# Two graph layers on one core: the last y tiles kept in SBUF, the first h turned in halves, the output stored by whole batches

## The chip, the core and the metric

The kernel runs on one core of a Trainium2 chip. The metric is the device time of one execution in microseconds. A core has TensorE (PE, with its weight loads shown as PEld), VectorE (DVE), ScalarE (ACT), GpSimd (POOL) and SyncE (SP); SP, ACT and POOL can issue DMAs. A tile in SBUF has 128 partitions; PE writes to PSUM banks of 128 x 512 float32.

## The reference

There are 16 graphs of 1024 nodes with 128 features, and a 0/1 adjacency matrix for each. Two blocks follow each other, both with a normalization in front and an addition of the input behind:

```python
# block 0: gated graph network, 4 layers
h = maximum(layernorm(x), 0)
for i in range(4):
    hw = h @ weight[i]                       # (b, n, c)
    m = einsum('bjn,bjd->bnd', adj, hw)      # sum over neighbours
    h = gru_cell(m, h, w_ih[i], w_hh[i], b_ih[i], b_hh[i])
x = x + h * nodemask
# block 1: graph convolution, 4 layers, batch norm over all batches and nodes
h = maximum(layernorm(x), 0)
for i in range(4):
    h = relu(einsum('bnm,bmc->bnc', adj, h @ W[i]) + b[i])
    mu, var = mean and variance of h over (b, n)
    h = gamma[i] * (h - mu) * rsqrt(var + 1e-5) + beta[i]
return x + h
```

In the GRU cell, r and z are sigmoids of sums of products with m and h, n is a tanh, and the new h is (1 - z) n + z h.

## The kernel before

The features lie transposed in SBUF, 128 features on the partitions and 1024 nodes along them. The large product, adjacency times features, is made exact enough by a split: a float32 operand is written as a high part, rounded to fp32r, and a low part, the rest; `aggregate_rows` (L523) multiplies both with each of eight rows of 128 nodes and accumulates in two PSUM banks. One batch and layer is 32 such matmuls of 128 x 512.

**Gated part.** Two streams, `sa` (even batches) and `sb` (odd), alternate by half steps: while one is in its gates, the other aggregates. Here every engine runs the instructions in the order in which they are written (`manual_schedule`). At the very start, batch 0's adjacency rows come by DMA and POOL (L562) or ACT (L560) rounds each one to fp32r; PE aggregates a row when it is rounded. In the same place the normalized y of batch 0 is turned by eight PE transposes into h (`turn`, L698, relu by ACT at L699), `open_gates` (L981) makes the first product with h, and `centred_high` (L779) writes the high part of the second half of y. A step of gates is `products` (L1011), `reset_gate` (r at L1029, DVE at L1030 and L1031), `candidate` (tanh, L1034), `update_gate` (z, L1038), `less`, `scaled` and `mixed` on DVE. In the first step `beside(0)` and `beside(1)` normalize and split batch 1 between them.

**Between the blocks.** For each batch the new x goes to DRAM (`store_xmid`, L743) and its normalized, rectified y too (`store_ymid`, L746). For the last two batches this work is done as chores during the first convolution layer: `chores` normalizes each stream's tile `s.xt` in place (L678) and stores it as y.

**Convolution part.** Outside `manual_schedule` the framework's scheduler orders the instructions. In layer 0, `load_y` (L1441) fetches a batch's y from DRAM into `feat[b]`, from batch 3 on behind a small POOL copy (L1440) that holds it back, and `first_split` splits it: ACT copies the high part (L1447), DVE subtracts (L1448). The split of batch b + 1 is issued while batch b aggregates. `first_weights` multiplies a batch's aggregate with the weights, `conv_done` applies bias and relu (L1421; in the last layer L1427) and takes the statistics (`bn_stats`, L1430). In layers 1 to 3 batch 0 is aggregated first on raw features (`raw_turned`, `raw_split`) while the factors of the batch norm are made (`affine`).

**Output.** In the last layer each relu writes `feat` in the order of the nodes, 256 elements an activation. `fetch_x` brings each x (L1530, POOL's queue) into 512-column halves of free tiles: the streams' tiles, the weights, and, at batch 15, the block of adjacency rows, one row tile and eight half tiles. The last loop normalizes a batch (L1643, L1647 or L1649), turns blocks of 128 columns on PE (L1655; nodes p * 4 + q of a half, a step of four columns), adds x on DVE (L1657) and stores each piece from SP (L1658). A piece of 512 nodes is one contiguous region of DRAM, 2 KB for each partition; batch 0 goes in pieces of 256, 256 and 512.

Of the kernel before, what the change touches and what calls it, by code (L numbers as in the profile page):

```python
# [8 lines left out]
F32 = mybir.dt.float32  # L9
F32R = mybir.dt.float32r  # L10
# [331 lines left out]
def exact_path(  # L342
# [36 lines left out]
    def acc(tag, name):  # L379
        return ps_m.tile([P, HALF], F32, tag=tag, name=name)  # L380

    def tmp(name):
        return ps_t.tile([P, HALF], F32, tag="tmp", name=name)
# [12 lines left out]
    def half_tile(name):  # L396
        return keep.tile([P, N], BF16, tag="half", name=name, bufs=8)
# [134 lines left out]
    with ExitStack() as st:  # L532
# [156 lines left out]
            norm_scale(nt, 0, NB)  # L689
            norm_blocks(xt, y, nt, range(NB))  # L690

        def turn(y, name, hT, func=AF.Copy):

            for hf in range(NH):
                pt = tmp(f"pt_{name}_{hf}")
                for q in range(BH):
                    k = hf * BH + q
                    nc.tensor.transpose(pt[:, q * P : (q + 1) * P], y[:, k * P : (k + 1) * P], ident)  # L698
                nc.scalar.activation(hT[:, hf * HALF : (hf + 1) * HALF], pt, func)  # L699
            return hT  # L700

        def by_nodes(cols):
            return cols.rearrange("c (q k i) -> c k q i", q=4, i=32)
# [39 lines left out]
        def store_ymid(b, y):  # L745
            nc.gpsimd.dma_start(ymid_d[b], y)  # L746
# [402 lines left out]
        with tc.manual_schedule(engines=every):  # L1149
# [53 lines left out]
            sa.centred_low(1)  # L1203
            for j in range(4):
                sa.rows[j] = first_round(0, j, raw0[j], nc.gpsimd)
            sa.agg_rows(range(4))
            for j in range(2):
                first_look(0, j, raw0[j])
            sa.rows[4] = first_round(0, 4, raw0[4], nc.scalar)
            sa.rows[5] = first_round(0, 5, raw0[5], nc.gpsimd)  # L1210
            turn(sa.y, "in0", h0, AF.Relu)
            sa.hT = h0
            first_look(0, 2, raw0[2])
            sa.agg_rows(range(4, 6))
            turn_small(*small_in)
            for j, eng in ((6, nc.scalar), (7, nc.gpsimd)):
                sa.rows[j] = first_round(0, j, raw0[j], eng)
            sa.open_gates()
            sa.agg_rows(range(6, NB))

            sb.sums(range(NB))
# [17 lines left out]
            def beside(hf):  # L1239
                sb.normed(range(hf * BH, (hf + 1) * BH))  # L1240
                sb.split_high(hf)
                sb.split_low(hf)
# [5 lines left out]

            sa.products(0)
            sa.reset_gate(0)  # L1250
            beside(0)
            in0 = turned_half(sb.y, h1, 0, "in1")
            exchange_in(in0, half_of(h1, 0))
            sa.candidate(0)
            sa.update_gate(0)
            sa.less(0)
            sa.scaled()
            beside(1)
# [154 lines left out]
    def conv_done(b, i, pm, stats, halfway=None):  # L1413
        for hf in range(NH):
            parts = 2 if halfway and hf else 1
            w = HALF // parts
            for k in range(parts):
                src = pm[hf][:, k * w : (k + 1) * w]
                if i < L - 1:
                    dst = feat[b][:, hf * HALF + k * w : hf * HALF + (k + 1) * w]  # L1420
                    last = nc.scalar.activation(dst, src, AF.Relu, bias=cvec(0, i))  # L1421
                else:
                    for q in range(w // (2 * P)):
                        u = hf * NH + k + q
                        dst = feat[b].rearrange("c (o j s i) -> c s o j i", o=2, j=4, s=4)[:, u]
                        part = src[:, q * 2 * P : (q + 1) * 2 * P].rearrange("c (j i o) -> c o j i", j=4, o=2)
                        last = nc.scalar.activation(dst, part, AF.Relu, bias=cvec(0, i))  # L1427
                    ks = slice(hf * NH + k, hf * NH + k + w // (2 * P))
                    dst = feat[b].rearrange("c (x s i) -> c x s i", s=4, i=32)[:, :, ks]
                nc.vector.bn_stats(stats[:, b * NH + hf + k, :], dst)  # L1430
            if halfway and hf == 0:
                sums = halfway()
        return sums if halfway else last
# [61 lines left out]
            nc.tensor.matmul(pc[hf], w_c[:, i, :], mt[:, cols], start=True, stop=True)  # L1495
        conv_done(0, i, pc, stats)

    xo = []

    def pieces(b):  # L1500

        return [(0, HALF // 2), (HALF // 2, HALF // 2), (HALF, HALF)] if b == 0 else [(0, HALF), (HALF, HALF)]

    def by_node(d, n0, n):

        return d[n0 : n0 + n, :].rearrange("(p q) c -> p q c", p=P)

    def xo_piece(b, n0, n):
        return xo[b][n0 // HALF][:, n0 % HALF : n0 % HALF + n].rearrange("p (q c) -> p q c", c=C)

    def fetch_x(b):

        first = len(xo)
        if b == 2:
            ts = [flat(f"xo{k}").rearrange("p k c -> p (k c)") for k in range(4)]
            hs = [t[:, k * HALF : (k + 1) * HALF] for t in ts for k in range(2)]
            for t in (w_hhT, w_mT):
                t = t.rearrange("p l c -> p (l c)")
                hs.extend(t[:, k * HALF : (k + 1) * HALF] for k in range(3))
        elif b == B - 1:  # L1520
            wide = turned_tile("xo_wide").rearrange("p a n -> p (a n)").bitcast(F32)
            row = keep.tile([P, N], F32, tag="row", name="xo_row", bufs=12)
            hs = [t[:, k * HALF : (k + 1) * HALF] for t, n in ((wide, 8), (row, 2)) for k in range(n)]
            hs.extend(half_tile(f"xo_h{k}").bitcast(F32) for k in range(8))
        else:
            return
        xo.extend(hs[k : k + 2] for k in range(0, len(hs), 2))
        for k in range(first, len(xo)):
            for n0, n in pieces(k):
                nc.gpsimd.dma_start(xo_piece(k, n0, n), by_node(xmid_d[k], n0, n))  # L1530

    def chores(s, b):

        xt, parts = s.xt, feat[b]
        y = xt.rearrange("p k c -> p (k c)")
        nt = norm_tiles(f"mid{b}")

        def sums(q):
            ks = range(2 * q, 2 * q + 2)
            masked_sum(b, xt, parts, ks)  # L1540
            norm_sums(xt, nt, ks)

        def factors():
            norm_factors(nt)
            store_xmid(b, xt)

        def blocks(hf):
            norm_blocks(xt, y, nt, range(hf * BH, (hf + 1) * BH))

        def fetch(seen):  # L1550
            nc.gpsimd.tensor_copy(parts[:, :1], seen[:, :1].bitcast(F32))
            pair_in(s.pair, parts, nc.gpsimd)

        return [
            (0, fetch),
            *((1 + q, lambda seen, q=q: sums(q)) for q in range(4)),
            (4, lambda seen: factors()),
            (6, lambda seen: blocks(0)),
            (7, lambda seen: blocks(1)),
            (7, lambda seen: store_ymid(b, y)),  # L1560
        ]

    late = {}
# [8 lines left out]
    for b in range(B):  # L1572
        if b == 1:
            with tc.issue_after(sb.last_dve.ins):
                rows = load_adjT(b, 0)
        else:
            rows = load_adjT(b, 0)
        yt = load_y(b + 1, hw_last if b > 2 else None) if b + 1 < B else None
        pm = banks(b, 0)
        aggregate(pm, hw, rows, 0)  # L1580
        behind = first_weights(*waiting, stats) if waiting else sb.last_m
        hw_next = first_split(b + 1, yt, behind) if b + 1 < B else None
        with tc.issue_after(split[0].ins), tc.issue_after(split[1].ins):
            for go in late.get(b, ()):
                go(hw[1])
        if b == B - 1:
            hw_next = raw_split(1)
        aggregate(pm, hw, rows, 1)
        if b == 12:
            raw_turned(1)  # L1590
        if b == 2:
            nc.gpsimd.dma_start(degree, degree_d.partition_broadcast(P))
        hw_last, hw, waiting = hw, hw_next, (b, pm)
# [46 lines left out]
    for b in range(B):  # L1640
        hT = work.tile([P, N], F32, tag="h", name=f"bn{b}_{L}", bufs=3)
        if b > 1:
            nc.scalar.activation(hT, feat[b], AF.Identity, bias=aff[1], scale=aff[0])  # L1643
        for n0, n in pieces(b):
            cols = slice(n0, n0 + n)
            if b == 0 and n0 == 0:
                nc.vector.tensor_scalar(hT[:, cols], feat[b][:, cols], aff[0], aff[1], ALU.mult, ALU.add)  # L1647
            elif b < 2:
                nc.scalar.activation(hT[:, cols], feat[b][:, cols], AF.Identity, bias=aff[1], scale=aff[0])  # L1649
            tag = turns[count % len(turns)]  # L1650
            count += 1
            pt = (tmp(f"pt_o{b}_{n0}") if tag == "tmp" else acc(tag, f"pt_o{b}_{n0}"))[:, :n]
            some = hT[:, n0 : n0 + n].rearrange("c (p q) -> c q p", p=P)
            for q in range(n // P):
                nc.tensor.transpose(pt[:, q * P : (q + 1) * P], some[:, q, :], ident)  # L1655
            xh = xo_piece(b, n0, n)
            nc.vector.tensor_add(xh, pt.rearrange("p (q c) -> p q c", c=C), xh)  # L1657
            nc.sync.dma_start(by_node(out[b], n0, n), xh)  # L1658


@with_exitstack
# [49 lines left out]
```

## Time and profile before

| what | value |
|---|---|
| median of 3 runs | 1768.21 us (1767.53 to 1768.83) |
| the profiled execution | 1769.41 us |
| its span, first to last instruction | 1767.6 us |
| mean granted PE clock | 0.996 |
| busy: PE, PEld | 1744.3 us (99%), 1185.0 us (67%) |
| busy: DVE, ACT, POOL | 1323.2, 1148.2, 398.2 us |
| DMA | 375.50 MB, mean 212 GB/s |

The gated part lasts until about 1150 us, the four convolution layers until about 1736 us, the output until the end. The busy time of PE is modelled from pipelined matmuls, so the waits of PE, the granted clock and the starts of successive matmuls say more than its share. A name such as `feat<-ymid_d` means that `feat` is written from `ymid_d`; "x16" counts instructions; what stands in brackets is the idle time before an instruction and what ended it.

### The profile page before, as it was taken

To read this page: it belongs to the slowest core of one execution; us is meant where nothing else is said; L and a number is where in the kernel's file an instruction comes from. 1 tells how busy PE (TensorE), PEld (TensorE's weight loads), DVE (VectorE), ACT (ScalarE), POOL (GpSimd) and SP (SyncE) were. 2 spreads that over 40 slices of the span, in tenths; PEclk is the share of its full clock that TensorE was granted. 3 is DMA by queue.
4 is the path that set the end of the run, shared out by engine and by line. 5 is a ranking of instruction groups with operands and counts; after the bars stand their busy time and mean duration, and the time that the engine had idled before them with its cause. 6 is when DMAs were issued, how large, how long until landed. Compare 5 with 4: busy or idle time off the path is not lost. (4 is left out here: it accounts for less than half of the span.)

```text
span 1767.6 us, 22191 instructions
## 1 busy us (share of the span) xinstructions
PE 1744.3 (99%) x6654; PEld 1185.0 (67%) x6654; DVE 1323.2 (75%) x2378; ACT 1148.2 (65%) x1821; POOL 398.2 (23%) x451
## 2 busy tenths in 40 slices
PE   9999999999999999999999999999999999999997
PEld 5665656565656565656656565677678888888886
DVE  7777887887887887887888686767566666666665
ACT  6567556657556656565655664468677778768765
POOL 4314223232341331331422423122200001000010
PEclk9999999999999999999999999999999999999999
DMA  8458379468557656746846836899957667757566
GB/s 287 128 139 275 101 159 289 118 172 257 160 161 213 196 154 193 238 129 178 259 122 172 288 102 182 270 323 323 344 178 238 236 241 238 261 204 265 212 236 254
DMA packets 305313, 375.50 MB, mean 212 GB/s; under 512 B 24876, under 2 KB 189520, under 8 KB 305184
## 3 DMA queue, kind: packets, MB, share of 16 engines
q1 hardware_dynamic: 292864, 334.06, 60.1%
q0 software_dynamic: 11792, 39.68, 7.0%
q8 instruction: 54, 0.88, 0.2%
q14 instruction: 75, 0.61, 0.1%
q10 hardware_dynamic: 528, 0.26, 0.0%
HBM read 272.19 MB, written 101.72 MB: 212 GB/s over the span
## 5 line engine op out<-in xcount | busy, mean ns | idle before, releaser
L523 PE MATMUL pm<-row,ghw 128*128 128x512 f32 x2048 | 504.2, 403 | 0.5 <-POOL row L562 0.3
L523 PEld LDWEIGHTS pm<-row,ghw 128*128 128x128 f32 x2048 | 383.8, 188 | 107.6 <-issue 23.7
L523 PE MATMUL pc_m<-wide,chw 128*128 128x512 f32 x1024 | 245.4, 395 | 0.0
L523 PEld LDWEIGHTS pc_m<-wide,chw 128*128 128x128 f32 x1024 | 190.5, 188 | 42.6 <-issue 4.3
L972 ACT COPY m<-pm 128x512 f32<-128x512 f32 x128 | 68.7, 588 | 229.6 <-PE pm L523 229.6
L587 POOL CAST row<-stage 128x1024 fp32r<-128x1024 f32 x112 | 127.4, 1143 | 339.3 <-DMA stage<-in_adj_dram 117.7
L523 PE MATMUL pc_g_r<-wide,chw 128*128 128x512 f32 x464 | 189.0, 407 | 6.5 <-ACT chw L1447 6.5
L523 PE MATMUL pc_g_z<-wide,chw 128*128 128x512 f32 x464 | 182.2, 393 | 0.0
L1030 DVE SCALAR_TENSOR_TENSOR r<-g_hn,vecs,r 128x512 f32<-128x512 f32 x128 | 93.4, 730 | 108.6 <-ACT r L1029 56.7
L633 POOL CAST pair<-row 128x1024 bf16<-128x1024 f32 x128 | 165.6, 1344 | 32.8 <-DVE adjT L639 32.8
L1034 ACT ACTIVATE r<-r,vecs 128x512 f32<-128x512 f32 x128 | 92.2, 720 | 115.5 <-DVE r L1031 113.3
L1368 DVE CAST wide<-block 128x1024 fp32r<-128x1024 bf16 x160 | 110.2, 694 | 68.4 <-PE pc_m L523 40.0
L1368 DVE CAST wide<-packed 128x1024 fp32r<-128x1024 bf16 x160 | 109.1, 689 | 62.9 <-PE pc_g_z L523 45.1
L1366 ACT CAST wide<-packed 128x1024 fp32r<-128x1024 bf16 x96 | 100.6, 1049 | 50.0 <-PE pc_m L523 20.8
L1011 PE MATMUL g_r<-m,w_mT 128*128 128x512 f32 x256 | 130.8, 592 | 0.1
L1011 PE MATMUL g_xn<-m,w_mT 128*128 128x512 f32 x256 | 130.7, 592 | 0.0
L1011 PE MATMUL g_z<-m,w_mT 128*128 128x512 f32 x256 | 130.7, 592 | 0.0
L1366 ACT CAST wide<-block 128x1024 fp32r<-128x1024 bf16 x96 | 100.5, 1048 | 43.7 <-PE pc_g_z L523 25.7
L1029 ACT ACTIVATE r<-g_r,brz 128x512 f32<-128x512 f32 x128 | 88.0, 687 | 58.2 <-PE g_r L1011 57.8
L1430 DVE BATCH_NORM_STATS2 stats<-feat 128x6 f32<-128x512 f32 x129 | 85.7, 684 | 49.0 <-ACT feat L1421 35.4
L1051 DVE TENSOR_TENSOR h<-h,z 128x512 f32<-128x512 f32 x128 | 95.2, 744 | 17.3 <-ACT z L1038 5.0
L1047 DVE TENSOR_TENSOR h<-h,r 128x512 f32<-128x512 f32 x96 | 72.0, 750 | 47.6 <-ACT r L1034 47.0
(202 smaller groups left out, 2904.0 us busy)
## 6 DMA issues: line engine op xcount, KB each, us to landing
block<-adjT_d SPq DMA_DIRECT2D x256, 256.0 KB, 4.7
packed<-adjT_d SPq DMA_DIRECT2D x256, 256.0 KB, 5.7
stage<-in_adj_dram SPq DMA_DIRECT2D x120, 512.0 KB, 5.2
adjT_d<-adjT SPq DMA_DIRECT2D x64, 512.0 KB, 7.2
cross_h<-t_h SPq DMA_DIRECT2D x94, 256.0 KB, 2.1
n_h<-cross_h SPq DMA_DIRECT2D x376, 64.0 KB, 2.1
xmid_d<-x POOLq DMA_DIRECT2D x16, 512.0 KB, 3.8
x<-in_x_dram SPq DMA_DIRECT2D x15, 512.0 KB, 4.4
```

The source lines that it names most:

```text
L523: nc.tensor.matmul(pm[hf], hw[s][:, j * P : (j + 1) * P], rows[j][:, hf * HALF : (hf + 1) * HALF], start=(j == 0 and s == 0), stop=(j == N ...
L587: nc.gpsimd.tensor_copy(t, stage[j % 4])
L633: nc.gpsimd.tensor_copy(halves[:, :, o], rows[4 * o + j].bitcast(F32))
L1011: nc.tensor.matmul(po, wT[:, i, g * C : (g + 1) * C], rhs, start=start, stop=stop)
L1029: nc.scalar.activation(r, pr, AF.Sigmoid, bias=brz[:, 3 * i : 3 * i + 1])
L1030: nc.vector.scalar_tensor_tensor(r, phn, b_hn(i), r, ALU.add, ALU.mult)
L1034: nc.scalar.activation(self.r, self.r, AF.Tanh, bias=b_in(self.i))
L1047: nc.vector.tensor_sub(ho, hin, self.r)
L1051: nc.vector.tensor_mul(ho, ho, self.z)
L1366: nc.scalar.copy(r, t)
L1368: nc.vector.tensor_copy(r, t)
L1430: nc.vector.bn_stats(stats[:, b * NH + hf + k, :], dst)
```

## The change

**y of the last two batches.** `store_ymid` is taken from the chores of batches 14 and 15, and `first_split` of these two reads the stream's own tile, in which y was made, in place of `feat[b]` loaded from DRAM. Batches 0 to 13 are as before.

**First h in halves.** `turn` becomes `turn_half`. PE's order at the start was rows 0 to 3, eight transposes, rows 4 and 5, the small transposes, `open_gates`, rows 6 and 7. It becomes rows 0 and 1, four transposes, row 2, `open_gates`, row 3, four transposes, rows 4 and 5, the small transposes, rows 6 and 7. On ACT the first relu of h now follows `centred_high(1)` directly and stands ahead of row 4's rounding. In the first step of gates z is computed right behind the reset gate, ahead of `beside(0)`, where it stood behind the candidate.

**Output in whole batches.** The relu of the last layer writes node p * 8 + r to column r * 128 + p, so its inner run of writes has a step of 128 elements (512 bytes), and `bn_stats` reads runs of four. The transposes then read 128 neighbouring columns. A partition holds 8 neighbouring nodes, 4 KB in DRAM. For batches 2 to 4 and 6 to 14 x is fetched and the result is stored with one DMA of 512 KB, after both halves are added; batches 0, 1, 5 and 15 still go in pieces, which are now parts (1 or 2 KB of each 4 KB run) of a batch. The tiles for x of batches 7 to 15 become four parts of the adjacency block, four row tiles and one split tile (`hw00`).

```diff
@@ start
+            sa.hT = h0
+            sa.agg_rows(range(2))
+            turn_half(sa.y, "in0", h0, 0, AF.Relu)
+            sa.agg_rows(range(2, 3))
+            sa.open_gates()
+            sa.agg_rows(range(3, 4))
-            sa.agg_rows(range(4))
...
-            turn(sa.y, "in0", h0, AF.Relu)
-            sa.hT = h0
+            turn_half(sa.y, "in0", h0, 1, AF.Relu)
...
-            sa.open_gates()
             sa.agg_rows(range(6, NB))
...
             sa.reset_gate(0)
+            sa.update_gate(0)
             beside(0)
...
             sa.candidate(0)
-            sa.update_gate(0)
             sa.less(0)
@@ conv_done, last layer
-                        dst = feat[b].rearrange("c (o j s i) -> c s o j i", o=2, j=4, s=4)[:, u]
-                        part = src[:, q * 2 * P : (q + 1) * 2 * P].rearrange("c (j i o) -> c o j i", j=4, o=2)
+                        dst = feat[b].rearrange("c (r o j s h) -> c s o j h r", r=8, o=2, j=4, s=4)[:, u]
+                        part = src[:, q * 2 * P : (q + 1) * 2 * P].rearrange("c (j h r o) -> c o j h r", j=4, r=8, o=2)
                         last = nc.scalar.activation(dst, part, AF.Relu, bias=cvec(0, i))
@@ output pieces
+    def whole(b):
+        return xo_whole[b] is not None and 1 < b < B - 1
+    def by_node(d, q0, n):
+        return d.rearrange("(p q) c -> p q c", p=P)[:, q0 : q0 + n, :]
@@ fetch_x
+            ts += [w3[:, :N], None, m3[:, HALF : 3 * HALF]]
...
+            ts = [wide[:, k * N : (k + 1) * N] for k in range(4)]
+            ts += [row_tile(f"xo_row{k}").bitcast(F32) for k in range(4)]
+            ts.append(keep.tile([P, N], F32R, tag="hw00", name="xo_hw").bitcast(F32))
...
+            if whole(k):
+                nc.gpsimd.dma_start(xo_whole[k].rearrange("p (q c) -> p q c", c=C), by_node(xmid_d[k], 0, NB))
+                continue
@@ chores
-            (7, lambda seen: store_ymid(b, y)),
@@ layer 0
-        yt = load_y(b + 1, hw_last if b > 2 else None) if b + 1 < B else None
+        if b + 1 < B - 2:
+            yt = load_y(b + 1, hw_last if b > 2 else None)
+        elif b + 1 < B:
+            yt = (sa if b + 1 == B - 2 else sb).xt.rearrange("p k c -> p (k c)")
@@ output loop
-            some = hT[:, n0 : n0 + n].rearrange("c (p q) -> c q p", p=P)
-            for q in range(n // P):
-                nc.tensor.transpose(pt[:, q * P : (q + 1) * P], some[:, q, :], ident)
+            for q in range(n):
+                nc.tensor.transpose(pt[:, q * P : (q + 1) * P], hT[:, (q0 + q) * P : (q0 + q + 1) * P], ident)
...
+            if not whole(b):
+                nc.sync.dma_start(by_node(out[b], q0, n), xh)
+        if whole(b):
+            nc.sync.dma_start(by_node(out[b], 0, NB), xo_whole[b].rearrange("p (q c) -> p q c", c=C))
```

More of the change, by code (lines that the diff above doesn't have):

```diff
@@ L690, in norm_apply, with turn_half @@
             norm_blocks(xt, y, nt, range(NB))
[L692 to L700, printed above, removed]
+        def turn_half(y, name, hT, hf, func=AF.Copy):
+            pt = tmp(f"pt_{name}_{hf}")
+            for q in range(BH):
+                k = hf * BH + q
+                nc.tensor.transpose(pt[:, q * P : (q + 1) * P], y[:, k * P : (k + 1) * P], ident)
+            nc.scalar.activation(hT[:, hf * HALF : (hf + 1) * HALF], pt, func)
         def by_nodes(cols):
@@ L1424, in conv_done @@
                         u = hf * NH + k + q
-                        dst = feat[b].rearrange("c (o j s i) -> c s o j i", o=2, j=4, s=4)[:, u]
-                        part = src[:, q * 2 * P : (q + 1) * 2 * P].rearrange("c (j i o) -> c o j i", j=4, o=2)
+                        dst = feat[b].rearrange("c (r o j s h) -> c s o j h r", r=8, o=2, j=4, s=4)[:, u]
+                        part = src[:, q * 2 * P : (q + 1) * 2 * P].rearrange("c (j h r o) -> c o j h r", j=4, r=8, o=2)
                         last = nc.scalar.activation(dst, part, AF.Relu, bias=cvec(0, i))
                     ks = slice(hf * NH + k, hf * NH + k + w // (2 * P))
-                    dst = feat[b].rearrange("c (x s i) -> c x s i", s=4, i=32)[:, :, ks]
+                    dst = feat[b].rearrange("c (x s h) -> c x s h", s=4, h=4)[:, :, ks]
                 nc.vector.bn_stats(stats[:, b * NH + hf + k, :], dst)
@@ L1496, in raw_weights, with xo_piece @@
         conv_done(0, i, pc, stats)
-    xo = []
+    xo, xo_whole = [], []
     def pieces(b):
[L1502 to L1509, printed above, removed]
+        return [(0, 2), (2, 2), (4, 4)] if b == 0 else [(0, 4), (4, 4)]
+    def whole(b):
+        return xo_whole[b] is not None and 1 < b < B - 1
+    def by_node(d, q0, n):
+        return d.rearrange("(p q) c -> p q c", p=P)[:, q0 : q0 + n, :]
+    def xo_piece(b, q0, n):
+        return xo[b][q0 // BH][:, q0 % BH * C : (q0 % BH + n) * C].rearrange("p (q c) -> p q c", c=C)
     def fetch_x(b):
@@ L1515, in fetch_x @@
             ts = [flat(f"xo{k}").rearrange("p k c -> p (k c)") for k in range(4)]
[L1516 to L1519, printed above, removed]
+            w3, m3 = (t.rearrange("p l c -> p (l c)") for t in (w_hhT, w_mT))
+            ts += [w3[:, :N], None, m3[:, HALF : 3 * HALF]]
+            apart = [w3[:, N : 3 * HALF], m3[:, :HALF]]
         elif b == B - 1:
             wide = turned_tile("xo_wide").rearrange("p a n -> p (a n)").bitcast(F32)
-            row = keep.tile([P, N], F32, tag="row", name="xo_row", bufs=12)
-            hs = [t[:, k * HALF : (k + 1) * HALF] for t, n in ((wide, 8), (row, 2)) for k in range(n)]
-            hs.extend(half_tile(f"xo_h{k}").bitcast(F32) for k in range(8))
+            ts = [wide[:, k * N : (k + 1) * N] for k in range(4)]
+            ts += [row_tile(f"xo_row{k}").bitcast(F32) for k in range(4)]
+            ts.append(keep.tile([P, N], F32R, tag="hw00", name="xo_hw").bitcast(F32))
         else:
             return
-        xo.extend(hs[k : k + 2] for k in range(0, len(hs), 2))
+        for t in ts:
+            xo_whole.append(t)
+            xo.append([t[:, :HALF], t[:, HALF:]] if t is not None else apart)
         for k in range(first, len(xo)):
-            for n0, n in pieces(k):
-                nc.gpsimd.dma_start(xo_piece(k, n0, n), by_node(xmid_d[k], n0, n))
+            if whole(k):
+                nc.gpsimd.dma_start(xo_whole[k].rearrange("p (q c) -> p q c", c=C), by_node(xmid_d[k], 0, NB))
+                continue
+            for q0, n in pieces(k):
+                nc.gpsimd.dma_start(xo_piece(k, q0, n), by_node(xmid_d[k], q0, n))
     def chores(s, b):
@@ L1643, in exact_path @@
             nc.scalar.activation(hT, feat[b], AF.Identity, bias=aff[1], scale=aff[0])
-        for n0, n in pieces(b):
-            cols = slice(n0, n0 + n)
-            if b == 0 and n0 == 0:
+        for q0, n in pieces(b):
+            cols = slice(q0 * P, (q0 + n) * P)
+            if b == 0 and q0 == 0:
                 nc.vector.tensor_scalar(hT[:, cols], feat[b][:, cols], aff[0], aff[1], ALU.mult, ALU.add)
@@ L1651, in exact_path @@
             count += 1
-            pt = (tmp(f"pt_o{b}_{n0}") if tag == "tmp" else acc(tag, f"pt_o{b}_{n0}"))[:, :n]
-            some = hT[:, n0 : n0 + n].rearrange("c (p q) -> c q p", p=P)
-            for q in range(n // P):
-                nc.tensor.transpose(pt[:, q * P : (q + 1) * P], some[:, q, :], ident)
-            xh = xo_piece(b, n0, n)
+            pt = (tmp(f"pt_o{b}_{q0}") if tag == "tmp" else acc(tag, f"pt_o{b}_{q0}"))[:, : n * P]
+            for q in range(n):
+                nc.tensor.transpose(pt[:, q * P : (q + 1) * P], hT[:, (q0 + q) * P : (q0 + q + 1) * P], ident)
+            xh = xo_piece(b, q0, n)
             nc.vector.tensor_add(xh, pt.rearrange("p (q c) -> p q c", c=C), xh)
-            nc.sync.dma_start(by_node(out[b], n0, n), xh)
+            if not whole(b):
+                nc.sync.dma_start(by_node(out[b], q0, n), xh)
+        if whole(b):
+            nc.sync.dma_start(by_node(out[b], 0, NB), xo_whole[b].rearrange("p (q c) -> p q c", c=C))
 @with_exitstack
```

## The prediction

> **What bounds the kernel now.** I read the list of waits of TensorE (PE) first. PE is busy for 1744.3 of 1767.6 us, so a change pays where PE waits, at the very start, or after its last instruction. Columns: who waits, on what, us in total, times, longest.
>
> ```profile
> PE pc_g_r L523 <- ACT chw L1447: 6.5, 1, 6.5
> PE pt_idle L1156 <- POOL ident masks.py:199: 2.4, 1, 2.4
> PE pt_wm L488 <- ACT w_both L482: 0.7, 1, 0.7
> PE g_z L1011 <- ACT z L1038: 0.6, 1, 0.6
> ```
>
> Two belong to the change: a single wait of 6.5 us for the split `chw` of L1447, and 0.6 us for the update gate `z`. The first I followed through the timelines of PE, ACT and POOL (start, length, engine, line, what; in brackets the idle time before):
>
> ```profile
> 1265.62 1.04 ACT L1447 CAST chw<-feat 128x1024 fp32r<-128x1024 f32 x1
> 1266.56 1.65 ACT L678 ACTIVATE x<-x,ms_mid,rs_mid 128x128 f32<-128x128 f32 x4
> 1268.51 1.02 POOL L746 DMA_DIRECT2D ymid_d<-x  x1 [8.71 <-ACT x L678]
> 1278.14 0.53 POOL L1441 DMA_DIRECT2D feat<-ymid_d  x1 [8.62 <-DMA ymid_d<-x]
> 1283.11 1.04 ACT L1447 CAST chw<-feat 128x1024 fp32r<-128x1024 f32 x1 [8.36 <-DMA feat<-ymid_d]
> 1273.46 4.24 PE L523 MATMUL pc_m<-wide,chw 128*128 128x512 f32 x16
> 1284.21 0.80 PE L523 MATMUL pc_g_r<-wide,chw 128*128 128x512 f32 x1 [6.51 <-ACT chw L1447]
> ```
>
> L1447 runs 16 times; the one at 1283.11 is batch 15's. Its y is finished in SBUF at 1268.2, goes out to DRAM (9.6 us), comes back (5.0 us), and only then is split. Batch 14's split, at 1265.62, is on time. Stages of the granted clock (columns: stretch, us, busy us of PE, PEld, DVE, ACT, POOL, then PEclk, DMA share, GB/s) show a second cost, PE at half speed after the wait:
>
> ```profile
> 1283.00:1284.00 1.00, 0.00 (x0) 0.00 (x0) 0.00 (x0) 0.89 (x1) 0.00 (x0) 0.50 0.05 20
> 1286.00:1288.00 2.00, 2.00 (x6) 1.54 (x5) 1.84 (x4) 2.00 (x4) 0.00 (x0) 0.50 0.00 0
> 1289.00:1290.00 1.00, 1.00 (x5) 0.81 (x4) 0.30 (x2) 0.00 (x0) 0.00 (x0) 0.85 0.00 0
> ```
>
> The same table for the output, and the DMA queue's packets in 1744 to 1760 and, behind, for one lone ymid store in 1089.3 to 1096:
>
> ```profile
> 1738.00:1740.00 2.00, 2.00 (x12) 1.66 (x12) 1.68 (x4) 2.00 (x3) 0.00 (x0) 1.00 0.39 131
> 1746.00:1748.00 2.00, 2.00 (x16) 1.82 (x15) 2.00 (x5) 2.00 (x3) 0.00 (x0) 1.00 1.01 379
> 1758.00:1760.00 2.00, 0.00 (x0) 0.00 (x0) 0.15 (x1) 0.00 (x0) 0.00 (x0) 1.00 1.02 378
> q1 hardware_dynamic: 3218, 5.85, 97.8%
> q0 software_dynamic: 144, 0.52, 19.7%
> ```
>
> The DMA engines have room until about 1744, then none until about 1761; DVE makes its last addition at 1758.2. So the end is set by the rate of the output stores.
>
> **y of the last two batches.** Two stores, two loads and two 0.24 us gate copies on POOL go; the splits read the tile where y was normalized. Batch 14's round trip is hidden and gains nothing. For batch 15 y is ready at 1268.2, and ACT is free after the relu that ends at 1274.75. With the cadence of the batches before (split 9.02 us after the last one) it starts at 1274.64; DVE's low part follows 1.34 us later and takes 1.22 (till 1277.20). PE wants it, by the step from 1255.41 to 1259.49 two batches earlier, at 1273.46 + 4.08 = 1277.54. It came at 1284.21: 6.67 us late. Eleven steps of the matmuls behind it, 1284.21 to 1289.40, took 5.19 us; at the usual 0.2275 us they take 2.50. So 2.69 us more went on the clock, 9.36 together.
>
> What is late next? Rows: the casts for (layer 1, batch 1) come 9.36 earlier, at 1284.45; their loads are issued by 1275.6 and landed within a median 7.9 us, 1283.5, with the round trip's traffic still beside them. raw_split reads loads issued before 1248. POOL's two fetches into the streams' tiles now wait for the splits (1268.2, 1277.2); queued behind is at most raw_split's load, some 2 us of delay if the order fell badly. I take 9.36, bounds 8.0 and 9.6.
>
> The Trainium skill ("TensorE: Matmul & The Clock Gate", section "Part 1: The HAM clock gate") lets a throttled clock recover after about 3.4 us of sustained work. By that the slow stretch would cost about 1.7 us and the sum would be 1 us smaller; the rows here show the half clock for 4.9 us, and I keep them.
>
> **The head.** Nothing is added; eight transposes, two relus and one product move, and `z` passes ahead of batch 1's first half. PE now idles between rows 0 to 3 (casts on POOL end 1.28 us apart), and the four transposes (about 0.5 us) fit there. But the first relu of h stands on ACT behind a relu that waits for DVE:
>
> ```profile
> 13.62 0.63 ACT L779 ACTIVATE ghw<-y_in 128x512 fp32r<-128x512 f32 x1 [2.90 <-DVE y_in L773]
> 20.42 1.07 ACT L972 COPY m<-pm 128x512 f32<-128x512 f32 x2 [3.09 <-PE pm L523]
> ```
>
> So open_gates cannot start before 14.15 + 0.55 = 14.7. PE is through with row 2 at about 13.3 and waits 1.45 us, with row 3 (13.56 before) queued behind. Row 3 then comes at 15.6, 2.04 later; 0.5 (transposes) and 0.86 (g_hn, two halves of 0.43) are done by then, leaving some 0.6 us late; I take 0.5 for the end of the sum. ACT works without a gap from 20.4 to 38.4, so all of it shifts by 0.5. Against that, PE's 0.6 us of waiting for `z` goes: `z` follows `r`. Its 0.67 us is then in front of batch 1's norm and splits, needed for row 4 at about 34.1, where the low split would end at about 34.0. Batch 1's `m` copies follow ACT's 0.5, with 0.23 us of slack. Net: 0.1 us gained, bounds 0.9 gained (if the relu of h isn't late) and 0.8 lost. The gap of 1.45 us costs no clock: after 1756.4 PE was idle over 3.5 us before the clock fell.
>
> **The last relu.** 64 activations write with a step of 512 bytes. No ACT row of before has one. Now they take 0.475 us (256 elements; 0.213 per 256 by L1643 against L1649, the rest fixed). The nearest rows are mild: ACT's L1401 reads every second element at 856 against L1649's 800 ns, PE's L1655 loads weights with a step of 16 bytes at 210 against L498's 191. I take a tenth, 0.05 each; bounds nothing and, at four times the element time, 0.64. Beside PE this is hidden: in 1610 to 1720 ACT is busy 7.02 us per batch of 9.09. On the path lie the last two: 0.1, at most 1.3. bn_stats reads whole runs still; nothing.
>
> **The output.** Per packet: 0.978 x 16 x 16.0 us / 3218 = 77.8 ns at 2 KB, 0.197 x 16 x 6.7 / 144 = 147 ns at 4 KB. A 256 KB piece (144 packets with its semaphores) holds the engines for 0.70 us, a whole batch in 4 KB runs for 1.32 instead of 1.40. Twelve batches go whole (2 to 4, 6 to 14): 0.96 us gained. Batch 2's first bytes wait for its second half, one addition of 0.61, while the engines have room: lost. Net 0.35 gained; bounds 1.9 gained (packets at the 440 GB/s of single slots) and 0.6 lost (no faster at all). PE's transposes now read without a step, SP issues 21 stores for 33, the fetches of x become fewer and start until 1727; DVE's additions and the queue cover them, and x arrives some 8 us before use.
>
> **Sum.** 9.36 + 0.1 + 0.35 - 0.1 = 9.7. The profiled execution took 1769.41 (span 1767.6 and 1.8 around it): 1759.7. It stood 1.20 above the median of 1768.21, so **1758.5**.
>
> **Rivals.**
> - *The wait moves.* Batch 15's split gets a new neighbour on ACT, or row casts come late: a wait of 2 to 3 us, too short for the clock to fall. For: the stage is replanned, DMA is 0.99 busy in 1268 to 1276. Against: the margins above. 1761.
> - *The relu becomes ACT's bound, and no gain is left.* At four times the element time (1.11 us) ACT needs 2.56 more per batch with 2.07 free: 0.49 x 15 = 7.4, plus 1.3 at the end: 1767.1.
> - *The same, and slower.* It decides beyond 1.19 us an activation: 15 x (4d - 2.07) + 2d reaches 13.2 us, the gain and 0.2%, at d = 0.71. At five times (1.33 us) it takes 20 + 1.7 us: 1780. For: nothing shows that step on ACT. Against: steps of 8 and 16 bytes cost 7 to 11%.
> - *It doesn't do what it says:* another wait of the same length holds batch 15's split. Nothing else of it is unfinished at 1274; 1768.
>
> The Trainium skill ("Advanced Engine Details and Errata", section "SBUF Cachelines") says that accesses which hit a new 16-byte line each time pay a penalty. That is the rule by which the relu rivals would come; it gives no size, and the 16-byte step on PE cost 19 ns of 191.
>
> **Numbers.** Forecast 0.82, moved wait 0.08, relu without gain 0.03, relu slower 0.04, no effect 0.03. Bounds added up give 1755.8 to 1762.4; the range is 1755.5 to 1763.5. About 0.2% (3.5 us) is what can be told from no change: faster 0.90, same 0.06, slower 0.04.
>
> **What would show it.** PE's wait for L1447 is gone and the clock stays at 1.00 near 1277. L1427 stays near 0.5 us. PE waits about 1.4 us for h near 13.3, and not for `z`. Output packets are 4 KB, and the last store lands 5 to 6 us after DVE's last addition, as before. I am wrong if the split still waits, if L1427 passes 1 us, or if the head grows by over 1 us.

## The result and the profile after

| | before | after |
|---|---|---|
| median of 5 runs | 1768.21 us (1767.53 to 1768.86) | 1759.38 us (1758.68 to 1760.17) |
| ratio | | 0.995, interval 0.9936 to 0.9965 |
| the profiled execution, its span | 1769.41, 1767.6 us | 1759.38, 1757.6 us |
| mean granted PE clock | 0.996 | 0.998 |

The change makes the kernel faster by 8.83 us (interval 6.2 to 11.3). The profiled pair differs by 10.0 us. PE's list of waits, after (who waits, on what, us in total, times, longest):

```profile
PE pt_idle L1152 <- POOL ident masks.py:199: 2.4, 1, 2.4
PE g_hn L977 <- ACT h_in L698: 1.4, 1, 1.4
PE pt_wm L488 <- ACT w_both L482: 0.7, 1, 0.7
```

The 6.5 us for the split is gone, and so is the 0.6 us for `z`. A wait of 1.4 us for the first half of h is new. The timelines of ACT and PE, after (start, length, engine, line, what; in brackets the idle time before; L1446 is L1447 of before, L977 is in `open_gates`):

```profile
1274.04 1.04 ACT L1446 CAST chw<-x 128x1024 fp32r<-128x1024 f32 x1
1272.85 4.24 PE L523 MATMUL pc_m<-wide,chw 128*128 128x512 f32 x16
1276.93 0.39 PE L523 MATMUL pc_g_r<-wide,chw 128*128 128x512 f32 x1
1285.96 1.98 PE L523 MATMUL pc_m<-wide,chw 128*128 128x512 f32 x8
14.65 1.13 PE L977 MATMUL g_hn<-h_in,w_hhT 128*128 128x512 f32 x2 [1.36 <-ACT h_in L698]
21.08 1.07 ACT L968 COPY m<-pm 128x512 f32<-128x512 f32 x2 [2.36 <-PE pm L523]
```

Batch 15's split now reads `x`, the stream's own tile, at 1274.04, where it ran at 1283.11. PE goes from batch 14's last 16 matmuls to batch 15's first in 1276.93 - 1272.85 = 4.08 us, with no idle time. The fourth line is the start of layer 1: 13.11 us after 1272.85. I call this the stretch. Before, it ran from 1273.46, which the prediction shows, to 1295.95, 22.49 us:

```profile
1295.95 1.98 PE L523 MATMUL pc_m<-wide,chw 128*128 128x512 f32 x8
```

So 9.38 of the pair's 10 us lie here. The stages after (us, busy us of PE, PEld, DVE, ACT, POOL, then PEclk, DMA share, GB/s):

```profile
1277.00:1279.00 2.00, 2.00 (x11) 1.65 (x10) 1.69 (x4) 2.00 (x5) 0.42 (x1) 1.00 0.84 245
1742.00:1744.00 2.00, 1.92 (x16) 1.47 (x15) 2.00 (x4) 2.00 (x3) 0.00 (x0) 1.00 1.02 408
1748.00:1750.00 2.00, 0.00 (x0) 0.00 (x0) 0.45 (x1) 0.00 (x0) 0.00 (x0) 1.00 1.01 391
```

The clock stays at 1.00 where batch 15 begins. In the output the DMA engines are as full as before but move 391 to 408 GB/s, against 378 and 379 in the two full rows shown of before. The last relu, before (L1427) and after (L1426; duration in ns, minimum/median/maximum):

```profile
L1427 ACT ACTIVATE feat<-pc_m,vecs x28: 466/475/485, 1617.9 to 1727.7; 128x256 f32<-128x256 f32 x28
L1426 ACT ACTIVATE feat<-pc_m,vecs x28: 673/690/724, 1608.0 to 1718.1; 128x256 f32<-128x256 f32 x28
```

The median went from 475 to 690 ns. What is paid for it on the path can be read at the end of the last layer. From the start of the last group of matmuls to the first normalization it is 1720.29 to 1727.02, 6.73 us, against 1730.23 to 1736.63, 6.40 us. From the first normalization to the end of the span it is 30.58 us against 30.97.

### The profile page after: what moved, and what is told of

Its sections match the earlier page's. It is cut to its first block, busy times and chain, and to the rows that moved or that the text cites. A ratio compares the mean times of both kernels' runs of the same rounds, so it can differ in the third digit from the quotient of the medians.

```text
span 1757.6 us, 22131 instructions
## 1 busy us (share of the span) xinstructions
PE 1739.6 (99%) x6654; PEld 1180.9 (67%) x6654; DVE 1319.9 (75%) x2378; ACT 1154.9 (66%) x1821; POOL 386.4 (22%) x433
```

## The experiments

The first four were timed beside one set of runs of the kernel before (median 1768.74 us), the other four beside another (1769.24 us).

**y of the last two batches alone, on the kernel before.**

```diff
-            (7, lambda seen: store_ymid(b, y)),
...
+        if b + 1 < B - 2:
+            yt = load_y(b + 1, hw_last if b > 2 else None)
+        elif b + 1 < B:
+            yt = (sa if b + 1 == B - 2 else sb).xt.rearrange("p k c -> p (k c)")
```

> The kernel before with the y part alone: batches 14 and 15 split from the streams' tiles. Theory: the whole gain sits here, the wait of 6.7 us and 2.7 us of half clock behind it, so 9.4 us under the kernel before (about 1758.8). Rival, that the parts share the gain (less DMA traffic in the output and a shorter head carry some of it): 6 to 7 us under it (about 1761.5), with the clock still low near 1284.

Measured: 1759.84 us, ratio 0.9943 (0.993 to 0.9957). From its PE timeline:

```profile
1273.48 4.24 PE L523 MATMUL pc_m<-wide,chw 128*128 128x512 f32 x16
1286.58 1.98 PE L523 MATMUL pc_m<-wide,chw 128*128 128x512 f32 x8
```

The stretch is 13.10 us, as with the whole change, and no other wait has come in its place. Against the runs beside it (1768.74 us) the median is 8.90 us lower, so this part alone gives all of the gain that the medians can tell.

**Only batch 14 from its tile.**

```diff
+            *([(7, lambda seen: store_ymid(b, y))] if b == B - 1 else []),
...
+        if b + 1 == B - 2:
+            yt = sa.xt.rearrange("p k c -> p (k c)")
+        elif b + 1 < B:
+            yt = load_y(b + 1, hw_last if b > 2 else None)
```

> The kernel before with batch 14 alone split from its stream's tile; batch 15 goes through DRAM as before. Theory: batch 14 was on time, so nothing moves (1768.2, within 1 us), and PE still waits 6.5 us for the split of batch 15. Rival, that the trip of batch 15 was slowed by the traffic of 14: the wait shrinks by 1 us or more.

Measured: 1769.44 us, ratio 1.0001 (0.9992 to 1.001). Its PE timeline, and its stages behind the wait:

```profile
1285.65 0.79 PE L523 MATMUL pc_g_r<-wide,chw 128*128 128x512 f32 x1 [6.86 <-ACT chw L1447]
1296.26 1.98 PE L523 MATMUL pc_m<-wide,chw 128*128 128x512 f32 x8
```

```profile
1288.00:1289.00 1.00, 1.00 (x2) 0.34 (x1) 0.41 (x1) 0.39 (x1) 0.00 (x0) 0.60 0.00 0
1289.00:1290.00 1.00, 1.00 (x5) 0.66 (x4) 0.67 (x1) 0.66 (x2) 0.00 (x0) 1.00 0.00 0
```

Batch 14's round trip was hidden: without it the wait is still there, and it has not shrunk (6.86 us for 6.51). The median lies 0.7 us above that of the runs beside it, which the interval can't tell from nothing. The rows also show what one profile could not. Here the clock is back some 3.2 us after the work starts (1285.65 to about 1288.8); in the profile of before it took 5.1 (1284.21 to about 1289.3; the prediction says 4.9), in those of two more kernels below 3.7 (the head alone) and 3.8 (the output alone). The order of the work differs a little too: in this kernel the four products of `first_weights` run at half clock right behind the first two matmuls, at 1286.66, and in the others behind the first sixteen.

**PE kept at work through the wait.** The kernel before, with transposes of the identity between batch 14's last matmul and batch 15's first.

```diff
+        if b == B - 1:
+            pt = tmp("pt_warm")
+            with tc.issue_after(last_mm.ins):
+                for k in range(56):
+                    warm = nc.tensor.transpose(pt[:, k % 4 * P : (k % 4 + 1) * P], ident, ident)
+            with tc.issue_after(warm.ins):
+                aggregate(pm, hw, rows, 0)
```

> The kernel before with 56 idle transposes on PE (about 6.1 us, results unused) between the last matmul of batch 14 and the first of batch 15, where PE waits. They fill the wait and do not remove it. Theory: the clock stays at full speed and the 2.7 us of half clock behind the wait go: 1765.5. Rival, that the slow matmuls after the wait come from rows or splits arriving one by one: no change, 1768.2, with the matmuls still 0.43 us apart.

Measured: 1766.75 us, ratio 0.9983 (0.9974 to 0.9992). PE's timeline and one stage:

```profile
1273.82 4.24 PE L523 MATMUL pc_m<-wide,chw 128*128 128x512 f32 x16
1277.90 6.28 PE L1585 MATMUL pt_warm<-ident 128*128 128x128 f32 x56
1283.93 0.48 PE L523 MATMUL pc_g_r<-wide,chw 128*128 128x512 f32 x1
1293.48 1.98 PE L523 MATMUL pc_m<-wide,chw 128*128 128x512 f32 x8
```

```profile
1284.00:1286.00 2.00, 1.86 (x9) 1.25 (x8) 2.00 (x4) 2.00 (x5) 0.00 (x0) 1.00 0.00 0
```

The split still comes late, 6.03 us behind the 1273.82 + 4.08 at which PE wants it, but the clock is 1.00. The stretch is 1293.48 - 1273.82 = 19.66 us, 2.83 less than before; 0.64 of that is a shorter wait, and 2.19 lie behind it. So the half clock is a cost by its own, beside the wait, and the rival is out. The median is 2.0 us under that of the runs beside it (1768.74), not 2.7. Also at full clock the stretch lost 0.52 us behind the wait (19.66 - 13.11 - 6.03): the matmuls start 0.54 us apart where the low part of the split comes late (1284.24 to 1284.78). So the 2.69 us of the prediction are not all the clock's.

**The output part alone, on the kernel before.** The edit is the last relu's two views, `whole`, `by_node`, `fetch_x` and the output loop of the diff above.

> The kernel before with the output part alone (node order by the last relu, whole batches). Theory: relu 0.475 to 0.69 us costs 0.35 us on the path to the last statistics, larger packets bring back 0.4 us behind it: no change within 0.5 us of 1768.2. Rival, that whole batches bring the DMA engines over 1 us: 1767 or less, with the time from the last factors to the end shorter by over 1 us.

Measured: 1768.46 us, ratio 1.0001 (0.9992 to 1.001). The relu's medians are 684 to 712 ns, and the path to the first normalization is 6.73 us, as in after. From there to the end it is 30.35 us, 0.62 less than before. The two nearly cancel.

**The head alone, on the kernel before.** The edit is the hunk "start" of the diff above.

> The kernel before with the head part alone (h turned in halves, the first gate step's z moved up). Theory: two opposite effects of about 0.6 us, a wait of 1.4 us for the relu of h on PE and the wait for z taken away; batch 0's sum ends 0.6 us later, the start of the gates of batch 0, layer 1 (57.39 us before) moves by less than 0.3 us; 1768.2 within 1 us. Rival, that the head shortens as a whole: that start comes over 0.6 us earlier.

Measured: 1768.85 us, ratio 1.0001 (0.9992 to 1.001). PE waits 1.13 us for h at 14.66, and batch 0's second gates start at 57.57, against 57.39 before.

**The first relu of h ahead of the split of y's second half, on the kernel after.** ACT runs in written order, so the relu no longer stands behind a relu that waits for DVE.

```diff
-            sa.centred_high(1)
-            sa.centred_low(1)
...
             turn_half(sa.y, "in0", h0, 0, AF.Relu)
+            sa.centred_high(1)
+            sa.centred_low(1)
```

> The changed kernel with one order turned on ACT and DVE: the relu of the first half of h stands ahead of the high and low split of the second half of y. Theory: the relu waited on ACT behind the split, which waits for DVE until 13.5 us. Without that PE's wait of 1.4 us before open_gates is gone, batch 0's sum (first copy of m, 21.08 us) ends 0.8 to 1.6 us earlier, and the start of batch 0's second gates (57.56 us) comes 0.5 to 1.3 us earlier: about 1758.5. Rival, that the last row, rounded at 18.3 us, or ACT holds it: m earlier, but the second gates within 0.3 us of 57.56.

Measured: 1758.65 us, ratio to before 0.9941 (0.9927 to 0.9954). From its PE timeline:

```profile
13.43 1.05 PE L977 MATMUL g_hn<-h_in,w_hhT 128*128 128x512 f32 x2
56.35 1.02 PE L1007 MATMUL g_r<-h,w_hhT 128*128 128x512 f32 x2
```

The wait for h is gone, and the second gates start at 56.35 instead of 57.56, 1.21 us earlier. In the trace that is the gain that the change's own order of the head missed. Whether it reaches the end isn't shown: at batch 14's last 16 matmuls 0.68 us of it is left (1272.17 for 1272.85), and the interval of the ratio overlaps that of the change.

**Whole batches, but the relu in plain order.** The kernel after, where the relu writes runs as in before and the transposes read every eighth column instead. The views of `bn_stats` and of the first two batches' normalization follow that order.

```diff
-                        dst = feat[b].rearrange("c (r o j s h) -> c s o j h r", r=8, o=2, j=4, s=4)[:, u]
+                        dst = feat[b].rearrange("c (o j s i) -> c s o j i", o=2, j=4, s=4)[:, u]
...
-                nc.tensor.transpose(pt[:, q * P : (q + 1) * P], hT[:, (q0 + q) * P : (q0 + q + 1) * P], ident)
+                nc.tensor.transpose(pt[:, q * P : (q + 1) * P], hT.rearrange("c (p q) -> c q p", q=NB)[:, q0 + q, :], ident)
```

> The changed kernel with the relu of the last layer writing in plain node order again; the transposes of the output read columns with a step of eight instead, and whole batches stay. Theory: the relu's 0.69 us is twice the time an element and comes from the 512-byte step of its writes; it falls back to 0.475, and 0.35 us go from the path between the last matmul and the last factors. The step on PE makes a weight load 210 ns or a little more, beside DVE's 1.22 us a batch: hidden. About 1759.0. Rival, that the step then limits PE: the output's pace rises over 1.3 us a batch and the time by over 1 us.

Measured: 1759.48 us, ratio 0.9944 (0.9931 to 0.9958). Its last relu:

```profile
L1426 ACT ACTIVATE feat<-pc_m,vecs x28: 466/475/485, 1608.7 to 1718.4; 128x256 f32<-128x256 f32 x28
```

It is back at 475 ns, and the path to the first normalization at 1727.39 - 1721.00 = 6.39 us, 0.34 shorter than in after. The transposes with a step do not slow the output: 29.61 us from the first normalization to the end. In the medians 0.34 us can't be told.

**Both of the last two.**

> The changed kernel with both orders: the relu of h first, and the step on PE. Theory: the two add up, 0.35 us at the end and 0.5 to 1.3 us at the start: about 1758.2, some 10 us under the kernel before. Rival, that the start's part is given back in the gated part: within 0.5 us of the changed kernel's 1759.4.

Measured: 1757.98 us (1756.96 to 1759.8), ratio 0.9936 (0.9922 to 0.995), the lowest median of all, beside the same set as the three before it. In its trace the second gates start at 56.55 and the path to the first normalization is 6.4 us, so both steps add up there. The interval overlaps that of after, so the medians alone don't show that it is better.

## Why the prediction came out as it did

The forecast of 1758.5 us was 0.9 us short of the 1759.38 measured, in sign and mechanism right. Term by term:

**y of the last two batches: right in the profiled pair (9.38 for 9.36), too large for a usual run.** Each point came as worked out: the split straight after ACT's relu (1274.04, for 1274.64 forecast in a run that was 0.6 later), PE's step of 4.08 us, no late row casts, nothing new in the wait's place. But the cost of the stall is not a fixed number. Five profiles, one each of five kernels, have the split late; "wait" is how much later than 4.08 us PE got it, "rest" is what the stretch lost beyond that, against the 13.11 us without a stall:

| kernel | batch 14's last 16 start | layer 1 starts | stretch | wait | rest |
|---|---|---|---|---|---|
| before | 1273.46 | 1295.95 | 22.49 | 6.67 | 2.71 |
| batch 14 only | 1274.55 | 1296.26 | 21.71 | 7.02 | 1.58 |
| head only | 1273.33 | 1294.97 | 21.64 | 6.44 | 2.09 |
| output only | 1272.90 | 1293.82 | 20.92 | 5.68 | 2.13 |
| kept at work | 1273.82 | 1293.48 | 19.66 | 6.03 | 0.52 |

Over the four without idle transposes the stall costs 7.81 to 9.38 us, mean 8.58, of which the rest is 2.13. With the clock held at 1.00 a rest of 0.52 stays, so by that one profile some 1.6 us of the 2.13 are the clock's, and the 2.69 that the prediction put down to the clock held some 0.5 of something else. The profile of before was the dearest of the four. These are different kernels, but one kernel's executions differ as well: of the 42 runs of the kernel before that were timed beside the experiments, one had a mean granted clock of 0.997 (1767.26 us), 36 had 0.996 (mean 1768.97) and five 0.995 (mean 1771.02).

So by these profiles the term was too large for a usual run, by 0.8 us, and the final step with it. The prediction took 1.20 us off because the profiled execution of before stood that much above its median, as if the execution after would stand as high. It stood on its own median. If the mean of the four is the usual stall, 0.8 of the 1.20 was the stall itself, which the change removes. The medians fit this (8.83), but their interval is too wide to prove it, and there is another reading: the two sets beside the experiments have medians of 1768.74 and 1769.24, so part of the 1.20 may be a low median of few runs. The two are not separated.

The Trainium skill ("TensorE: Matmul & The Clock Gate", section "Part 1: The HAM clock gate") has the clock come back after about 3.4 us of sustained work, with a window that runs on by itself, so that the moment differs from run to run. The prediction set that aside for the 4.9 us of one profile. The four profiles show 3.2, 3.7, 3.8 and 5.1 us: three agree with the page to half a microsecond, and the one that the prediction went by is the odd one. The clock's share of some 1.6 us is nearer to the 1.7 us that the prediction estimated from the page than to the 2.69 used.

**The head: 0.1 us gained was forecast; the traces show some 0.2 lost, and the medians can't tell it.** The steps came true: no wait for `z`, `open_gates` at 14.65 (forecast 14.7) after a wait of 1.36 us (1.45), the end of the sum 0.66 us later (0.5). Batch 0's second gates start at 57.56, 57.57 and 57.66 in the three kernels with this head and at 57.10 to 57.79, mean 57.40, in the five without it. The mean is 0.2 us later, where 0.1 earlier was forecast, inside the scatter of the five. The two opposite effects can be told apart at the first copy of m, which ends batch 0's sum. The copy starts at 21.08, 21.08 and 21.15 with this head and at 20.09 to 20.78, mean 20.40, without: 0.70 us lost, for 0.5 forecast. From it to the second gates it is 36.48 to 36.51 us with this head and 36.97 to 37.01 without, and there the two groups lie clear of each other: 0.5 us gained, where PE's wait for `z` is gone, for 0.6 forecast. Of the pair, the stretch from there to batch 14's last 16 matmuls is 0.78 us shorter after, and no part of the change lies in it. That point scatters too, 1272.90 to 1274.55 over the kernels without the head's change, so no more than chance need be behind it.

**The last relu: the mis-sized term.** 0.05 us was added to each activation by rows with steps of 8 and 16 bytes; it was 0.215, once more the 0.213 us that 256 elements take. It doubled the time per element, within the bounds of 0 and 0.64. One of the two rows that made the step look mild was read against the wrong neighbour: the 210 ns of a PE load with a step of 16 bytes were set beside L498's 191, which is a load for a product. Loads for transposes of neighbouring columns were in the same profile (mean ns behind the comma), and the transposes of the output themselves, after, take as long:

```profile
L1655 PEld LDWEIGHTS pt_o<-ident,bn 128*128 128x128 f32 x128 | 16.8, 210 | 3.1 <-PE pt_idle_end L1636 0.8 <-ACT bn L1643 0.6 <-ACT bn L1649 0.3
L1636 PEld LDWEIGHTS pt_idle_end<-ident 128*128 128x128 f32 x24 | 2.7, 140 | 0.1
L1662 PEld LDWEIGHTS pt_o<-ident,bn 128*128 128x128 f32 x128 | 13.7, 141 | 6.4 <-ACT bn L1651 4.3 <-PE pt_idle_end L1644 1.1 <-ACT bn L1657 1.0
```

So that step cost 69 ns on 141, half as much again, and not 19 on 191. On the path it is 0.33 us for 0.1. The kernel with plain runs, at 475 ns and 6.39 us, shows that the step of the writes is the cause. Beside PE the relu stayed hidden, as forecast: from the start of layer 1 to the last group of matmuls it is 434.33 us after and 434.28 before. So neither rival about the relu came near. The Trainium skill ("Advanced Engine Details and Errata", section "SBUF Cachelines") says that a new 16-byte line at each access is paid for. The rows agree for ACT's writes with a step of 512 bytes: 690 ns for 475. No run here shows where between 4 and 512 bytes the price of a write begins.

**The output: 0.35 us gained forecast, 0.39 in the pair.** Five kernels with half-batch stores take 30.84 to 31.01 us from the first normalization to the end; five with whole batches take 29.61 to 30.58. The gain is there in each, at 0.26 to 1.4 us between the ends of the two, and the DMA engines still set the end.

**Sum.** With the stall at its mean, 8.58 - 0.33 + 0.39 and a head of -0.2 give 8.4 us; the medians differ by 8.83. In the profiled pair the sum of 9.7 came close to the 10.0 measured, and some of that is luck: 9.38 - 0.33 + 0.39 make 9.4, and the other 0.6 us are there because batch 14's last 16 matmuls start 0.61 us earlier in the profile of after, which no part of the change explains. The range's slow end was also added up wrongly: with the slow bounds of the four terms (8.0, -0.8, -1.3, -0.6) the sum is 5.3 us, which makes 1762.9 and not 1762.4. The stated range holds both.

## What to carry to other kernels

A value that is still in SBUF should not go through DRAM to reach its next reader: here it was one batch in sixteen, and the round trip cost PE its clock as well as its time. Before a stall is costed from one profile, look at the same stall in others: this one moved by 1.6 us between four profiles, and an offset from the median may be the very thing that the change removes. When an instruction is moved forward on an engine that runs in written order, look at what it now stands behind: the first relu of h, put ahead of an instruction that waits for DVE, brought the second gates 1.2 us earlier in the trace, which the move alone did not. When a price is taken from the nearest row, compare that row with one that differs from it in the step alone.

## What the hardware showed beyond what was expected

- ACT's writes with a step of 512 bytes take twice the time per element: 690 ns for 475 at 256 float32 elements in after, 684 in the kernel with the output part alone and in the one with the relu of h first, and 475 again where the writes go back to runs.
- PE's loads of transposed blocks took 141 ns from neighbouring columns (after), 194 ns with a step of eight columns (whole batches, but the relu in plain order) and 210 ns with a step of four (before). The longer step is the cheaper one.
- Idle transposes are enough to hold the clock at 1.00 through a wait: 56 of them in 6.28 us, and the matmuls behind them ran without the half clock.
